# A four-layer network on one core: column sums added to the skip term by DMA, and the last experts in two halves

## The chip, the core and the metric

One core of a Trainium2 chip runs the whole program in one launch. The engines are PE (TensorE: matmuls), DVE (VectorE), ACT (ScalarE), POOL (GpSimd) and SP (SyncE, which here only issues DMAs). Each works through its own queue in order. The metric is the device time of one execution in microseconds (us), median of several runs.

## The reference, cut to what matters

The input x is 4 images of 64 x 64 positions with 128 channels. Four layers follow; each adds to x. Two are touched.

Layer 0 runs a selective scan over the 4096 positions of an image in four directions (rows, columns, and both backwards) for 256 inner channels with 16 states each, and sums the four results:

```python
xa = jax.nn.silu(xc)                       # after a 3 x 3 depthwise convolution
xs = jnp.stack([x_flat, x_t, jnp.flip(x_flat, 1), jnp.flip(x_t, 1)], axis=1)
ys = _selective_scan(xs, dts4, A, Bp4, Cp4, D_param, b_dt)   # each adds u * D_param
y = ys[:, 0] + transpose(ys[:, 1]) + flip(ys[:, 2]) + transpose(flip(ys[:, 3]))
y = layer_norm(y) * ln_w + ln_b
y = y * jax.nn.silu(z)
return y @ w_out
```

The four directions each add u times D_param, so their sum has a skip term of 4 D_param times xa. The column sums are the two transposed directions, the row sums the other two.

Layer 3 is a windowed attention with a layer norm, and then a mixture of 8 experts: router_probs = softmax(x @ router_w + router_b), the best two of eight are kept, and each token gets their weighted sum of x @ expert_w + expert_b.

## The kernel before

The program is written in the order of its Python code. Inside the layers' main loops the order on PE, ACT and DVE is the order of the code; POOL and SP are placed by a scheduler. A generator holds work that goes beside a main loop: each `yield` hands back to it.

**Layer 0.** The main loop has 512 steps: 4 images (b), 2 halves of the inner channels (h), 64 chunks (c) of 64 positions. A step does, for all four directions, the products (`products`, L641, PE, into three PSUM buffers db), the carry of the step before added to their first column (L654, DVE), four scans (L657, DVE; state in a buffer big), the carry for the next step (L665, POOL), the product with C over all states (L673, POOL, two per step), and the sum over the states (`total`, L686 on PE; with the results of the second half of the chunks, the direction that came first is added by L698). ACT copies the sums into two SBUF tiles (L705): yr for the two row directions, yc for the two column directions, each 128 x 4096 floats for one half of the channels. `inputs` (L632, DVE) prepares the next step and needs `delta` (L621, PE), which shares the tile aux with the sums. `fetch` loads ct, xo and dg for two steps ahead; SP issues these.

The row sums yr are written to DRAM eight chunks at a time (L710), once their second visit is through. A column chunk touches every row of yc, so yc goes out whole at the end of a half, in two writes of 1 MB (L714) to a DRAM tensor yc_d. yr and yc are single buffers.

Beside the loop of image b run, from chunk 4 of its first half, one after the other:

- `back(b - 1)`: 8 blocks of 512 positions. It loads the column sums yc, the skip term y0, the row sums yr and the gate zs (`fetched`, L459, 512 KB each, four buffers t4k), adds y2 += y0 (L468, POOL), y += y2 (L472, POOL), normalises, multiplies with the gate (L505, POOL), and projects (L512). The last image's `back` runs beside the beginning of layer 1.
- `front(b + 1)` and `middle(b + 1)`: group norm, input projection, convolution (L370), silu (L380, ACT, giving xh), the skip term y0 = xh * 4 D_param (L382, POOL, written to DRAM by L385), transposes and the scan's inputs. For image 0 these two run alone, ahead of the loop.

**Layer 3.** The main loop is the attention of the four images. Two lists of generators run beside it: `light` (the `front` and `back` of an image) and `heavy` (`chosen`, the router and experts of an image, two halves of 16 tiles each by `some`). `step` advances the first generator of a list. When an image's attention is done, `passed` runs its `back`, which writes blocks of t, and then appends that image's `chosen` to `heavy`; `chosen` of the last image comes after all else:

```python
            while light or heavy:
                step(light)
                step(heavy)
            for _ in chosen(B - 1, free_bank):
                pass
```

The router's logits are L2074, the experts' matmuls L2145, their weighted sums L2151 (DVE). `back`'s last operation of a block is L2037. Three kinds of PSUM banks are used: `own_bank` (tile x, one buffer), `shared_bank` (mm, two) and `free_bank` (s, two).

Of the kernel before, what the change touches and what calls it, by code (L numbers as in the profile page):

```python
# [15 lines left out]
B = 4  # L16
# [42 lines left out]
def tl(pool, shape, tag, dtype=F32, bufs=None):  # L59
    return pool.tile(shape, dtype, name=tag, tag=tag, bufs=bufs)  # L60
# [99 lines left out]
def layer0(cm, x, W, x1, also, kept):  # L160
# [5 lines left out]
    with ExitStack() as ctx:  # L166
# [93 lines left out]
        def begin(b):  # L260
            img[b] = {
                "zs": tl(dr, [P, 2, S], "zs"),
                "dl": tl(dr, [2, P, S], "dl_d"),
                "ct": tl(dr, [NST, S], "ct_d"),
                "xT": tl(dr, [2, S, P], "xT_d"),
                "y0": tl(dr, [P, 2, S], "y0_d"),
                "yr": tl(dr, [P, 2, S], "yr_d"),
                "yc": tl(dr, [P, 2, S], "yc_d"),
            }


# [87 lines left out]
        def middle(b, bank, pool, tag, ahead):  # L359

            ready = [shifted(i, pool, tag) for i in range(ahead)]
            for k in range(NBLK):
                cols = slice(k * BLK, (k + 1) * BLK)
                xa = []
                for h in range(2):
                    ps = bank()
                    x3 = ready.pop(0)
                    for dx in range(3):
                        for g in range(4):
                            nc.tensor.matmul(  # L370
                                ps[g * CG : (g + 1) * CG, :], lhsT=cdiag[:, 4 * h + g, dx, :],
                                rhs=x3[:, g, 0 : 8 * PADW].rearrange(
                                    "p (r w) -> p r w", w=PADW
                                )[:, :, dx : dx + HW],
                                start=(dx == 0), stop=(dx == 2),
                            )
                    if 2 * k + h + ahead < 2 * NBLK:
                        ready.append(shifted(2 * k + h + ahead, pool, tag))
                    xh = tl(tmp, [P, BLK], "t2k")
                    nc.scalar.activation(xh, ps, AF.Silu, bias=vec[:, 0, h : h + 1])  # L380
                    y0 = tl(tmp, [P, BLK], "t2k")
                    nc.gpsimd.tensor_tensor(  # L382
                        y0, xh, d4[:, h : h + 1].to_broadcast([P, BLK]), ALU.mult
                    )
                    nc.sync.dma_start(img[b]["y0"][:, h, cols], y0)  # L385
                    xa.append(xh)
                    yield
                    ps = bank()
                    for i in range(4):
                        nc.tensor.transpose(  # L390
                            ps[:, i * P : (i + 1) * P], xa[h][:, i * P : (i + 1) * P], cm.ident
                        )
                    t = tl(tmp, [P, 4, P], "t2k")
                    nc.scalar.copy(t, ps.rearrange("p (t c) -> p t c", c=P))
                    nc.sync.dma_start(
                        img[b]["xT"][h, cols, :].rearrange("(t p) c -> p t c", p=P), t
                    )
                    yield
                    if h == 0:
                        yield  # L400
                        yield
                ps = bank()
                n = RANK + 2 * NST
                for h in range(2):
                    nc.tensor.matmul(
                        ps[0:n, :], lhsT=w_xp[:, h, :], rhs=xa[h], start=(h == 0), stop=(h == 1)
                    )
                xd = tl(tmp, [P, BLK], "t2k")
                nc.scalar.copy(xd[0:n, :], ps[0:n, :])
                xr = tl(tmp, [P, 8, TC], "t2k")  # L410
                nc.scalar.copy(
                    xr[0:n], ps[0:n, :].rearrange("p (c t) -> p c t", t=TC)[:, :, ::-1]
                )
                nc.sync.dma_start(img[b]["ct"][:, cols], xd[RANK + NST : n, :])
                yield
                ps = bank()
                pb = ps[:, 0 : 8 * NST].rearrange("p (c n) -> p c n", n=NST)
                for c in range(8):
                    for j in range(2):
                        nc.tensor.matmul(  # L420
                            pb[j * TC : (j + 1) * TC, c, :],
                            lhsT=xr[0:n, c, :] if j else xd[0:n, c * TC : (c + 1) * TC],
                            rhs=cm.ident[0:n, RANK : RANK + NST], start=True, stop=True,
                        )
                nc.vector.tensor_copy(BT[:, 8 * k : 8 * k + 8, :], pb)
                for h in range(2):
                    yield


                    ps = bank()  # L430
                    nc.tensor.matmul(
                        ps, lhsT=w_dt[:, h * P : (h + 1) * P], rhs=xd[0:RANK, :],
                        start=True, stop=True,
                    )
                    bias = vec[:, 1, h : h + 1]
                    u = tl(tmp, [P, BLK], "t2k")
                    r = tl(tmp, [P, BLK], "t2k")
                    nc.scalar.activation(u, ps, AF.Abs, bias=bias)
                    nc.scalar.activation(r, ps, AF.Relu, bias=bias)
                    nc.scalar.activation(u, u, AF.Exp, scale=-1.0)  # L440
                    nc.scalar.activation(ps, u, AF.Identity, bias=cm.ones[:, 0:1])
                    v = tl(tmp, [P, BLK], "t2k")
                    nc.scalar.activation(v, ps, AF.Ln)
                    yield
                    nc.vector.scalar_tensor_tensor(
                        ps, ps, 1.0, u, ALU.subtract, ALU.subtract
                    )
                    nc.vector.tensor_tensor(ps, v, ps, ALU.subtract)
                    nc.vector.tensor_tensor(r, ps, r, ALU.add)
                    nc.sync.dma_start(img[b]["dl"][h, :, cols], r)  # L450
                yield

        def back(b, bank, tmp=tmp, t4=t4):


            def fetched(k, *names):
                ts = [tl(t4, [P, 2, BLK], "t4k") for _ in names]
                for t, name in zip(ts, names):
                    nc.sync.dma_start(t, img[b][name][:, :, k * BLK : (k + 1) * BLK])  # L459
                return ts  # L460

            y2, y0 = fetched(0, "yc", "y0")
            yield
            for k in range(NBLK):
                cols = slice(k * BLK, (k + 1) * BLK)
                xr = tokens(b, k, tmp)
                y, zl = fetched(k, "yr", "zs")
                nc.gpsimd.tensor_tensor(y2, y2, y0, ALU.add)  # L468
                yield
                yield  # L470
                yield
                nc.gpsimd.tensor_tensor(y, y, y2, ALU.add)  # L472
                if k + 1 < NBLK:
                    y2, y0 = fetched(k + 1, "yc", "y0")
                yield
                yield
                ps = bank()
# [202 lines left out]
        def total(I, part):  # L680
# [30 lines left out]
            if c == NCHUNK - 1:  # L711
                for r in range(2):
                    rows = slice(r * S // 2, (r + 1) * S // 2)
                    nc.sync.dma_start(img[b]["yc"][:, h, rows], yc[:, rows])  # L714

        def turn_bank():
            return tl(db, [P, BLK], "db")
# [886 lines left out]
def layer3(cm, W, M, cst, x2, out):  # L1604
# [6 lines left out]
    with ExitStack() as ctx:  # L1611
# [109 lines left out]
        def rows(a, b, k):  # L1721
            return a[b, k * BLK : (k + 1) * BLK, :].rearrange("(t p) c -> p t c", p=P)
# [273 lines left out]
        def back(b, bank):  # L1996
# [20 lines left out]
            for k in range(NBLK):  # L2017
# [18 lines left out]
                yield  # L2036
                nc.vector.tensor_tensor(t, t, xl, ALU.add)  # L2037
                nc.sync.dma_start(rows(me["t"], 0, k), t)
                if k + 1 < NBLK:
                    t, xl = block(x2, b, k + 1), block(me["xl"], 0, k + 1, "xl")  # L2040
                yield
# [131 lines left out]
        def passed(b, bank):  # L2173

            yield from back(b, bank)
            if b + 1 < B:
                heavy.append(chosen(b, own_bank))


        with tc.manual_schedule(engines={mybir.EngineType.PE}):  # L2180
            for _ in front(0, free_bank):
# [3 lines left out]
            for T in range(-AHEAD, LAST + 2):  # L2185
# [4 lines left out]
                for x in range(4):  # L2190
# [13 lines left out]
                    if x == 0 and 1 < T:  # L2204
                        divided(T - 2, 1)
                        b, m = divmod(T - 1, NM)
                        if m == 0:
                            merged(b - 1)
                            light.append(passed(b - 1, shared_bank if b < B else free_bank))
                            if b + 1 < B:  # L2210
                                fronts[b + 1] = front(b + 1, shared_bank)
                                light.append(fronts[b + 1])
# [3 lines left out]
                        weights(T, x // 2, x % 2)  # L2216
                    step(heavy)
                    step(light)
            while light or heavy:
                step(light)  # L2220
                step(heavy)
            for _ in chosen(B - 1, free_bank):
                pass


def hybrid_kernel(tc, I, cst, out):
# [86 lines left out]
```

## Time and profile before

| | |
|---|---|
| median of 3 runs | 11011.42 us (11002.11 to 11043.79) |
| the profiled execution | 11035.94 us, of which the span 11034.1 us |
| granted TensorE clock, mean | 0.892 |
| busy in the span: PE / DVE / ACT / POOL | 86% / 69% / 49% / 49% |
| scans L657 (DVE) | 2048 of 2286 ns |
| products L673 (POOL) | 1024 of 4538 ns |
| skip term L382 (POOL) | 64 of 1041 ns |
| adds L468 and L472 (POOL) | 32 each of about 2350 ns |

A span of 11 ms has stages with different limits: layer 0 fills the first 6430 us or so, layers 1 and 2 reach to about 9000, layer 3 takes the rest. A row of the page with a line gives engine, operation, out<-in, shapes and the count, then busy us and mean ns of one, then the idle time of the engine just before such instructions with what ended it.

### The profile page before, as it was taken

Reading aid. Unit: us, or ns where it says so; the run is one execution under the profiler, and the core shown is the slowest. Engines: PE = TensorE matmul, PEld = TensorE weight load, DVE = VectorE, ACT = ScalarE, POOL = GpSimd, SP = SyncE. Lnnn points to the kernel's source line nnn. Section 1 sums busy time; section 2 is a strip of 40 time slices with the busy share of each in tenths; the row PEclk is TensorE's granted clock in tenths of the full one; section 3 lists DMA queues with packets and bytes.
Section 4 is the critical chain, followed back from the end, with each engine's and each line's share of the span. In section 5 each row is a group of like instructions: output and inputs, shape, how many; then the busy total and the mean of one; then the engine's idle time right before and its main releaser. Section 6 shows DMA issues by size and latency. Waiting matters only on the chain. (4 is left out here: it accounts for less than half of the span.)

```text
span 11034.1 us, 163573 instructions
## 1 busy us (share of the span) xinstructions
PE 9541.3 (86%) x59368; PEld 4544.1 (41%) x59368; DVE 7577.1 (69%) x11174; ACT 5380.1 (49%) x13471; POOL 5453.8 (49%) x2661
## 2 busy tenths in 40 slices
PE   7789998889998889997889964999999966988886
PEld 2344444344443344443344432444444434544442
DVE  1898888888988888988899976645452122355546
ACT  5666443556444555445552223767777622343321
POOL 0678888878888888888889940000000000000000
PEclk7899999889998899998999976999999976677777
DMA  4334443334443334433333341111100065022101
GB/s 139 105 104 153 132 131 117 112 112 144 137 132 121 111 114 154 136 118 123 115 109 99 104 134 40 39 35 35 34 28 18 17 189 105 13 49 56 37 23 46
DMA packets 1479867, 1026.27 MB, mean 93 GB/s; under 512 B 698052, under 2 KB 1296808, under 8 KB 1474712
## 3 DMA queue, kind: packets, MB, share of 16 engines
q1 hardware_dynamic: 1479064, 1015.80, 31.0%
q8 instruction: 475, 7.78, 0.3%
q14 instruction: 328, 2.69, 0.1%
HBM read 683.79 MB, written 331.61 MB: 92 GB/s over the span
## 5 line engine op out<-in xcount | busy, mean ns | idle before, releaser
L657 DVE TENSOR_TENSOR_SCAN big<-dA,db 128x1024 f32<-128x1024 f32 x2048 | 4679.7, 2286 | 81.1 <-ACT dA L564 2.8
L673 POOL TENSOR_TENSOR big<-big,ct 128x2048 f32<-128x2048 f32 x1024 | 4647.0, 4538 | 84.5 <-DVE big L657 5.6
L641 PE MATMUL db<-dg,du 64*64 64x512 f32 x16384 | 2455.2, 621 | 98.3 <-DVE db L654 85.6
L686 PE MATMUL aux<-big,both 128*64 128x256 f32 x16384 | 2121.2, 403 | 466.1 <-DVE db L654 257.5
L686 PEld LDWEIGHTS aux<-big,both 128*64 128x64 f32 x16384 | 1207.8, 143 | 1466.8 <-issue 637.2
L705 ACT COPY yr<-aux 128x64 f32<-128x64 f32 x1024 | 226.2, 221 | 2773.2 <-PE aux L686 1316.5
L641 PEld LDWEIGHTS db<-dg,du 64*64 64x64 f32 x16384 | 748.2, 136 | 1329.1 <-issue 1225.9
L612 ACT ACTIVATE dg<-mask,BT 128x64 f32<-128x64 f32 x4096 | 1007.4, 341 | 4.8 <-DMA dg_d<-dg 4.8
L1443 PE MATMUL av<-e,x 128*128 128x512 f32 x2048 | 974.0, 592 | 4.6 <-ACT e L1438 4.6
L1394 PE MATMUL qk<-a,xT 128*128 128x512 f32 x2048 | 966.6, 594 | 8.7 <-ACT e L1398 7.9
L1398 ACT ACTIVATE e<-qk,nk 128x512 f32<-128x512 f32 x1024 | 693.2, 685 | 539.3 <-PE qk L1394 538.4
L564 ACT ACTIVATE dA<-dp,A 128x252 f32<-128x252 f32 x2048 | 870.6, 509 | 1.4
L973 POOL TENSOR_TENSOR g_rs<-g_rs,qrow 128x4 f32<-128x4 f32 x32 | 41.1, 1286 | 1499.8 <-DVE g_rs L972 1499.8
L665 POOL TENSOR_TENSOR cy<-big,a 128x32 f32<-128x32 f32 x1008 | 271.1, 269 | 758.7 <-DVE big L657 497.2
L1394 PEld LDWEIGHTS qk<-a,xT 128*128 128x128 f32 x2048 | 378.0, 190 | 462.3 <-issue 358.0
L1443 PEld LDWEIGHTS av<-e,x 128*128 128x128 f32 x2048 | 381.6, 190 | 434.8 <-issue 393.7
L1438 ACT ACTIVATE e<-e 128x1024 f32<-128x1024 f32 x510 | 538.8, 1056 | 15.5
L654 DVE TENSOR_TENSOR db<-db,cy 128x16 f32<-128x16 f32 x2016 | 336.2, 167 | 264.4 <-PE db L641 211.2
L1919 ACT ACTIVATE e<-s 72x576 f32<-72x576 f32 x448 | 273.6, 643 | 492.4 <-PE s L1912 489.6
L632 DVE TENSOR_TENSOR du<-xo,aux 128x128 f32<-128x128 f32 x1024 | 248.7, 283 | 346.3 <-PE aux L621 211.1
L1930 POOL COPY vp<-vt 72x160 f32<-72x160 f32 x56 | 20.2, 362 | 898.9 <-PE po L1936 896.2
L2151 DVE SCALAR_TENSOR_TENSOR tex<-x,gw,tex 128x128 f32<-128x128 f32 x768 | 264.4, 344 | 252.1 <-PE x L2145 237.0
(531 smaller groups left out, 11001.6 us busy)
## 6 DMA issues: line engine op xcount, KB each, us to landing
ct<-ct_d SPq DMA_DIRECT2D x1024, 128.0 KB
dg_d<-dg SPq DMA_DIRECT2D x256, 512.0 KB
dg<-dg_d SPq DMA_DIRECT2D x256, 512.0 KB
xo<-xT_d SPq DMA_DIRECT2D x2048, 32.0 KB
x<-xc_d SPq DMA_DIRECT2D x144, 264.0 KB
dp<-dl_d SPq DMA_DIRECT2D x256, 128.0 KB
t2k<-in_x SPq DMA_DIRECT2D x96, 256.0 KB
sp<-sp_d SPq DMA_DIRECT2D x16, 1280.0 KB
```

Of the source, the lines that this page charges most:

```text
L564: nc.scalar.activation(w["dA"][:, :, g, n, 1:], w["dp"][:, g, :, 1:], AF.Exp, scale=A[:, w["h"], g, n : n + 1],)
L612: nc.scalar.activation(q["dg"][:, n, :], mask, AF.Copy, scale=BT[:, q["c"], n : n + 1])
L641: nc.tensor.matmul(bs[j][p * TC : (p + 1) * TC, g * NH0 : (g + 1) * NH0, :], lhsT=q["du"][kp][half, g * TC : (g + 1) * TC], rhs=q["dg"][ha ...
L654: nc.vector.tensor_tensor(bs[j][:, :, 0], bs[j][:, :, 0], old[:, u, :], ALU.add)
L657: nc.vector.tensor_tensor_scan(st[:, u].rearrange("p n t -> p (n t)"), q["w"]["dA"][:, c % QC].rearrange("p g n t -> p (g n t)"), bs[j].re ...
L673: nc.gpsimd.tensor_tensor(sv, sv, q["ct"].rearrange("p n t -> p (n t)").unsqueeze(1) .to_broadcast([P, 4, NH0 * TC]), ALU.mult,)
L686: nc.tensor.matmul(yp[p * TC : (p + 1) * TC], lhsT=both, rhs=st[:, :, p * NH0 + n, :], start=(n == 0), stop=(n == NH0 - 1 and not late),)
L1394: nc.tensor.matmul(ps, lhsT=me["xT"][:, kt * P : (kt + 1) * P], rhs=me["a"][k], start=True, stop=True,)
L1398: nc.scalar.activation(e[:, j, :], ps, AF.Exp, bias=me["nk"][:, kt : kt + 1], scale=2.0)
L1438: nc.scalar.activation(es[g + 2], es[g + 2], AF.Exp)
L1443: nc.tensor.matmul(avs[b, k], lhsT=img[b]["x"][:, kt, :], rhs=e[:, j, :], start=(kt == 0), stop=(kt == NT - 1),)
L1919: nc.scalar.activation(e.rearrange("p j h q -> p j (h q)"), ss[p][0:HALF, :, 0 : 2 * WIN], AF.Exp, scale=0.5,)
```

## The change

In layer 0, the column sums are no longer written to a tensor of their own. GpSimd issues two accumulating DMAs of 1 MB that add yc onto the skip term y0 in DRAM, at the place in `total` where they were written. `back` loads y0 in place of both, and has one add. The skip term itself is made by ACT, as a copy with a scale for each partition.

In layer 3, `back` counts the blocks it has written in me["done"]. `last` goes into the heavy list once the main loop is through; it waits for half of the blocks of the last image, runs `some` on that half, and then does the same for the other. `back` of the last image takes its PSUM from `shared_bank` instead of `free_bank`.

```diff
@@ middle
-                    nc.gpsimd.tensor_tensor(
-                        y0, xh, d4[:, h : h + 1].to_broadcast([P, BLK]), ALU.mult
-                    )
+                    nc.scalar.activation(y0, xh, AF.Copy, scale=d4[:, h : h + 1])
                     nc.sync.dma_start(img[b]["y0"][:, h, cols], y0)
@@ back
-            y2, y0 = fetched(0, "yc", "y0")
+            (y0,) = fetched(0, "y0")
             yield
             for k in range(NBLK):
...
                 y, zl = fetched(k, "yr", "zs")
-                nc.gpsimd.tensor_tensor(y2, y2, y0, ALU.add)
                 yield
                 yield
                 yield
-                nc.gpsimd.tensor_tensor(y, y, y2, ALU.add)
+                nc.gpsimd.tensor_tensor(y, y, y0, ALU.add)
                 if k + 1 < NBLK:
-                    y2, y0 = fetched(k + 1, "yc", "y0")
+                    (y0,) = fetched(k + 1, "y0")
@@ total
             if c == NCHUNK - 1:
                 for r in range(2):
                     rows = slice(r * S // 2, (r + 1) * S // 2)
-                    nc.sync.dma_start(img[b]["yc"][:, h, rows], yc[:, rows])
+                    nc.gpsimd.dma_start(
+                        img[b]["y0"][:, h, rows], yc[:, rows], accum_op=ALU.add
+                    )
@@ layer 3, back
                 nc.sync.dma_start(rows(me["t"], 0, k), t)
+                me["done"] = k + 1
@@ layer 3
+        def last():
+            for half in range(2):
+                while img[B - 1].get("done", 0) < NB * (half + 1):
+                    yield
+                yield from some(img[B - 1]["t"], B - 1, NB * half, free_bank)
...
-                            light.append(passed(b - 1, shared_bank if b < B else free_bank))
+                            light.append(passed(b - 1, shared_bank))
...
+            heavy.append(last())
             while light or heavy:
                 step(light)
                 step(heavy)
-            for _ in chosen(B - 1, free_bank):
-                pass
```

## The prediction

> **What bounds the kernel now.** I first cut the span by stage. Layer 0 runs from 300 to about 6430 us, 58% of it. The page's slices show DVE and POOL as full as PE there, and two rows carry them:
>
> ```profile
> DVE  1898888888988888988899976645452122355546
> POOL 0678888878888888888889940000000000000000
> ...
> L657 DVE TENSOR_TENSOR_SCAN big<-dA,db 128x1024 f32<-128x1024 f32 x2048 | 4679.7, 2286 | 81.1 <-ACT dA L564 2.8
> L673 POOL TENSOR_TENSOR big<-big,ct 128x2048 f32<-128x2048 f32 x1024 | 4647.0, 4538 | 84.5 <-DVE big L657 5.6
> ```
>
> A step is four scans (9.1 us of DVE) and two L673 (9.1 us of POOL), so whatever delays either engine shows. Next, busy time by window: a stretch with nothing beside the scan, and one where `back` works on the image before (us, then PE, PEld, DVE, ACT, POOL busy):
>
> ```profile
> 5850.00:6350.00 500.00, 464.06 (x3496) 218.64 (x3496) 484.32 (x485) 110.63 (x444) 469.29 (x219) 1.00 0.33 101
> 2310.00:2346.00 36.00, 25.57 (x200) 13.10 (x201) 25.63 (x26) 15.11 (x63) 28.61 (x15) 0.86 0.34 110
> ```
>
> The plain stretch holds 195 scans, so a step takes 10.26 us and DVE idles 0.33 us in it. In the second DVE is busy for 25.6 of 36. What ends its idle time there is in the timeline of POOL and DVE:
>
> ```profile
> 2182.90 2.34 POOL L472 TENSOR_TENSOR t4k<-t4k 128x1024 f32<-128x1024 f32 x1 [4.37 <-DMA t4k<-yr_d]
> ...
> 2185.49 0.18 DVE L654 TENSOR_TENSOR db<-db,cy 128x16 f32<-128x16 f32 x1 [4.90 <-POOL cy L665]
> ...
> 2195.36 0.18 DVE L654 TENSOR_TENSOR db<-db,cy 128x16 f32<-128x16 f32 x1 [4.96 <-PE db L641]
> ```
>
> POOL is in order: L472 waits 4.37 us for its load, adds for 2.34, and the carry L665 behind it is late, so DVE waits. The second wait is the same delay by another way: L673 was late, hence PE's sums L686, and the products L641 queue behind those.
>
> Third, the steps where an image half ends (c = 1 and 2 of the next half):
>
> ```profile
> 2657.19 0.81 SPq L714 DMA_DIRECT2D yc_d<-yc  x2
> 2663.90 0.21 ACT L705 COPY yr<-aux 128x64 f32<-128x64 f32 x1 [11.39 <-DMA yr_d<-yr]
> 2668.80 0.27 ACT L705 COPY yc<-aux 128x64 f32<-128x64 f32 x1 [4.69 <-DMA yc_d<-yc]
> 2670.17 0.48 DVE L632 TENSOR_TENSOR du<-xo,aux 128x128 f32<-128x128 f32 x2 [9.47 <-PE aux L621]
> ```
>
> The next half may not overwrite yc before its 2 MB are out, and ACT, PE and DVE stand in line behind that. In the packet records, each 8 KB packet took 309 ns; all moved from 2661.4 to 2668.3.
>
> **What the Trainium skill says.** "DMA: Bandwidth & Descriptors", section "SWDGE vs HWDGE vs iDMA": an accumulating DMA can only be issued from GpSimd, whose software writes the descriptors. No DMA of POOL is in this trace. Same page, "SDMA does more than copy": the adder reduces two streams, 2048 elements at most. A row here has 2048; no run shows its speed. Same page, "Queues, rings and completion order": issuing engines have rings of their own, served in turn. The trace agrees as far as it goes: on SP's one queue, yc's packets waited 4 us behind earlier transfers.
>
> **The change, part by part.**
>
> *(a) One add of `back` less.* The order in which the changed program's instructions stand on POOL has the remaining add (y += y0) where L468 stood, except in an image's first two blocks (one step earlier, and L472's place of block 0). On SP, y0's load takes yc's place, yr's takes y0's, zs' takes yr's. So the remaining add waits for a load in L468's old position, behind the same ct loads: I keep L468's wait and drop L472 with its wait. Groups of instructions, 1800 to 5700 us (busy, mean ns, idle before):
>
> ```profile
> L468 POOL TENSOR_TENSOR t4k<-t4k 128x1024 f32<-128x1024 f32 x24 | 56.5, 2354 | 81.2 <-DMA t4k<-y_d 74.3 <-DMA xo<-xT_d 6.8
> L472 POOL TENSOR_TENSOR t4k<-t4k 128x1024 f32<-128x1024 f32 x24 | 56.3, 2346 | 32.2 <-DMA t4k<-yr_d 30.1 <-PE db L641 2.0
> ```
>
> Both hold POOL for 226 us over 24 blocks. DVE idles 194 us in the 36 steps that contain them; less 0.33 each, 182 are theirs, so 44 us (1.8 a block) are absorbed. Dropping L472's 88.5 frees 71 us in proportion, 88 if the slack is used up first. I take **-80**; the ends are -45 (only the adds go, since the later load rules) and -170 (both waits go: 56.5 less 44 stay).
>
> *(b) yc's write becomes 16 accumulating DMAs of 1 MB, by POOL.* They stand after the first L673 of c = 1, a step ahead of the stall. Two issues of an estimated 1 us (the skill's "Specifications" there gives this first-byte latency) delay the carry behind them, which is needed only after the stall: nothing. What counts is when yc comes free. In front of the second image's scan, SP issued the writes at 1823.6, the packets ran from 1829.1 to 1835.5, and ACT went on at 1836.4. In the new order POOL is free at 1825.5 (that step's L673), and an own ring need not wait behind yr and ct: data from about 1827.5. 16 rows for each of 16 engines: 4.9 us at 309 ns. The adder reads two streams, so I take twice the copy, 9.9 us; with 1.6 for sharing and 1.5 to completion, 1840.5, so +4 at each half. Seven such seams, and the end, where layer 1's first DVE instruction (L904) waits 20.2 us on yc's write: 8 x 4 = **+32**. Bounds: equal to a copy, -1 each (-8); five times a copy, 5 x 4 - 1 = +19 each (+152). Loads of y0 replace those of yc one for one in bytes; 24 of 512 KB fewer, against 16.8 MB read by the adder.
>
> *(c) The skip term by ACT.* 64 multiplications of 1.04 us leave POOL, 64 copies of about 0.63 us (row L488, same shape) join ACT. Per step of `middle` POOL has over 1 us free (busy 635 of 746 us, 2634 to 3380), nobody is listed as waiting for L382, and steps after one show no more DVE idle: 0. On ACT (busy 348 of those 746) the copy stands between L380 and a table load or L394; in the opening's 16 of them ACT idles 1.2 us there, waiting for PE's transposes. If that cover failed, 64 x 0.63 = +40. SP no longer stands 83 us in all before L385 for POOL, so ct and xo are issued earlier: **-5** (0 to -15).
>
> *(d) `back` of the last image, beside layer 1:* the same drop; PE waits 11.2 us for L472 there. **-6** (0 to -20).
>
> *(e) Layer 3.* `last` is behind `chosen` of image 2 in the heavy list, so it can begin early only if that ends before image 3's `back`. These two lines, one from the query of each source line, say no:
>
> ```profile
> L2037 DVE TENSOR_TENSOR tin<-tin,xl x32: 639/680/692, 9629.3 to 10845.4; 128x512 f32<-128x512 f32 x32
> ```
>
> ```profile
> L2145 PE MATMUL x<-ew,x3T x288: 592/697/1223, 10001.0 to 10855.9; 128*128 128x512 f32 x144
> ```
>
> `back` is through at 10845, the old experts run to 10856. In the changed order nothing of layer 3 moves on any engine; `back` merely writes bank mm instead of s, two buffers either way: **0** (3 either way).
>
> Sum: -80 + 32 - 5 - 6 = -59. The profiled execution took 11035.9 us (span 11034.1), 24.5 above the median 11011.4 of the runs; so 11035.9 - 59 = 10976.9 profiled, **10952** as a median. A measurement of this kernel tells about 0.5%, 55 us, from no change.
>
> **The rivals.**
> - *Both waits go.* With three tiles a block in four buffers, y0 and yr might land before POOL asks. For it: the boundary and the queue are less crowded. Against: the loads stand behind ct on SP, which waits on POOL. -170 + 32 - 11 = -149: 10862.
> - *The wait stays whole.* The one add waits for the later of two loads, and the shorter POOL queue arrives sooner and waits longer: -45 + 32 - 11 = -24: 10987.
> - *The adder is slow.* One row costs r copies; a seam moves by 5(r - 1) - 1 us. The 91 us gained in (a), (c) and (d) are spent at r = 3.5, and over that the kernel is slower, as ACT, PE and DVE all stand behind yc. r = 6: 8 x 24 = +192, so +101: 11112. For it: each row is read and written back in HBM beside the read from SBUF; against: rows of 8 KB are the largest here.
> - *Layer 3 does what its name says*: half of the tokens, about 85 us, would have to run under `back`. The order excludes it.
>
> **How the numbers follow.** Forecast 0.46, of which about 0.28 lies past -55 us (its own spread, from (a) at -71 to -88 and a seam of -1 to +9, is 10880 to 11000); both waits go 0.17; wait stays 0.13; slow adder 0.24, two thirds of it past +55, which begins at r = 4.9. So faster 0.28 + 0.17 = 0.45, slower 0.16, within 0.5% 0.39. The range takes in the second case nearly whole and the slow adder to r = 5 (+61): 10860 to 11070.
>
> **What would show it.** Right: 24 adds fewer on POOL in 1800 to 5700 us and the remaining one with 50 to 80 us of wait; steps with adds, now 16 to 20 us, fall by 3 on average; L632's waits at the seams grow from 5.4 to 9.8 us by about 4; packets of POOL's queue at some 620 ns; the time after 9000 us unchanged. Wrong: adder packets at 309 ns or above 1 us; DVE idle in the add steps unchanged; L2145 moved in the tail; ACT's copies with somebody waiting for them.

## The result, and the profile after

The changed kernel takes 10989.15 us (median of 20 runs; 11013.81 before): 0.9979 of the time before, 95% interval 0.9970 to 0.9989. That is 25 us less where 59 were forecast. The two profiled executions differ by 62 us, 10974.05 against 11035.94; most of that excess is scatter between single executions. The kernel with layer 3's part alone, which gains nothing in its median, has a profiled execution of 11011.80 us, 24 below that of before.

The page of the changed kernel, the two rows that fill layer 0, and the new queue:

```profile
L653 DVE TENSOR_TENSOR_SCAN big<-dA,db 128x1024 f32<-128x1024 f32 x2048 | 4680.0, 2286 | 82.1 <-ACT dA L560 3.2
L669 POOL TENSOR_TENSOR big<-big,ct 128x2048 f32<-128x2048 f32 x1024 | 4646.1, 4537 | 85.0 <-DVE big L653 5.4
...
q0 software_dynamic: 2304, 16.78, 0.7%
```

Scans and products are what they were. The queue of POOL's own DMAs holds the 16 accumulating ones, 16.78 MB. Busy time by window, a plain stretch and one around the last add of image 1 (us, then PE, PEld, DVE, ACT, POOL):

```profile
5800.00:6300.00 500.00, 462.97 (x3490) 218.04 (x3490) 483.87 (x488) 110.48 (x444) 468.99 (x221) 1.00 0.33 101
...
2283.00:2319.00 36.00, 31.67 (x241) 16.11 (x234) 29.87 (x32) 17.76 (x72) 31.24 (x16) 0.91 0.34 111
```

The plain stretch is unchanged. In the other, DVE is busy for 29.9 of 36 us, where it was 25.6. Groups of instructions, 1800 to 5700 us (busy, mean ns, idle before):

```profile
L468 POOL TENSOR_TENSOR t4k<-t4k 128x1024 f32<-128x1024 f32 x24 | 56.4, 2351 | 110.6 <-DMA t4k<-yr_d 80.4 <-issue 11.6 <-PE db L637 10.7
L501 POOL TENSOR_TENSOR t4k<-t4k 128x1024 f32<-128x1024 f32 x24 | 56.4, 2349 | 14.7 <-ACT t4k L497 14.7
```

24 adds are gone, but the 24 that remain wait 110.6 us, nearly as long as both kinds together did (113.4). The timeline at the second image's beginning (start, duration, then in brackets the idle time before and what ended it), before:

```profile
1823.59 0.90 SPq L714 DMA_DIRECT2D yc_d<-yc  x2
...
1836.40 0.27 ACT L705 COPY yc<-aux 128x64 f32<-128x64 f32 x1 [5.55 <-DMA yc_d<-yc]
...
1837.77 0.48 DVE L632 TENSOR_TENSOR du<-xo,aux 128x128 f32<-128x128 f32 x2 [6.40 <-PE aux L621]
```

And in the changed kernel:

```profile
1811.49 1.76 POOL L710 DMA_DIRECT2D y_d<-yc  x2
...
1828.73 0.27 ACT L701 COPY yc<-aux 128x64 f32<-128x64 f32 x1 [11.38 <-DMA y_d<-yc]
...
1830.10 0.48 DVE L628 TENSOR_TENSOR du<-xo,aux 128x128 f32<-128x128 f32 x2 [13.07 <-PE aux L617]
```

This seam (the step in which ACT waits for the write of yc at the start of a half) costs DVE 13.1 us, where it was 6.4. yc comes free 17.2 us after POOL issues, where it was 12.8 after SP did. The packet records of POOL's queue show 628 ns for each 8 KB packet (median), 2.03 times the plain write's 309. The tail, by source line:

```profile
L2035 DVE TENSOR_TENSOR tin<-tin,xl x32: 635/681/693, 9566.7 to 10783.3; 128x512 f32<-128x512 f32 x32
...
L2144 PE MATMUL x<-ew,x3T x306: 592/697/1222, 9899.7 to 10793.8; 128*128 128x512 f32 x153
```

The last operations of `back` and of the experts of the image before begin at 10783 and 10794 us, eleven microseconds apart as before. Layer 3 is what it was.

### The profile page after: what moved, and what is told of

Its sections match the earlier page's. It is cut to its first block, busy times and chain, and to the rows that moved or that the text cites. A ratio compares the mean times of both kernels' runs of the same rounds, so it can differ in the third digit from the quotient of the medians.

```text
span 10972.3 us, 163387 instructions
## 1 busy us (share of the span) xinstructions
PE 9474.1 (86%) x59368; PEld 4529.1 (41%) x59368; DVE 7569.2 (69%) x11174; ACT 5425.1 (49%) x13536; POOL 5331.9 (49%) x2581
## 3 DMA queue, kind: packets, MB, share of 16 engines
q0 software_dynamic: 2304, 16.78, 0.7%
```

## The experiments

Each kernel is compared with runs of the kernel before on its own chip (medians of before 11044, 11018 and 11027 us in the three groups), so a difference in us here is (1 - ratio) times that median. Step lengths are differences between the starts of every fourth scan. Images, blocks and steps are counted from 0, so that image 1 is the second; "over plain steps" means less 10.26 us.

**The skip term alone** (`middle` as in the change, all else as before).

> Only the skip term is moved from POOL to ACT; all else is the kernel before. Theory (from the two traces): the opening, where middle of image 0 runs alone, loses a round trip over POOL in each block, so the first scan begins near 282 us instead of 300 and the median falls by about 19 us; from the first scan to L904 nothing changes (6140 us, 3 either way). The prediction's view: the opening is unaffected, the whole change is worth 5 us. Rival: the 64 extra copies get in the way of ACT beside the scan, and the time from first scan to L904 grows by up to 40 us, so that the median is up to 20 us above before.

Measured: 1.0007 (0.9998 to 1.0016), 8 us more, in an interval that holds zero. My reading that the opening had become 19 us shorter falls: the first scan began at 279 us here, but at 282 us in the next kernel too, which leaves the skip term on POOL. The 300 us of the profile before were scatter: the single traces of later kernels began at 280 to 299 us with either engine.

**Layer 3 alone** (`last` and the bank).

> Only layer 3's part: last() in the heavy list, and back of the last image in bank mm. Theory: no instruction moves, so the median is that of before within 5 us and the time from L904 to the end is 4594 us, but for scatter of some 15 us. Rival: the changed kernel's profile is 20 us shorter from L904 to the end because of this part; then this kernel shows 10 to 20 us less in the median and in that stretch. Second rival: bank mm is shared with other work and costs, +10 to +20 us, which would explain why the median fell by 25 us only while layer 0 is 41 us shorter in the profile.

Measured: 1.0000 (0.9992 to 1.0008). No gain or loss is seen, to within 9 us. This kernel's layer 0 is that of before, so its trace serves as a second one of the old order. From the first DVE instruction of layer 1 to the end it took 4581 us (4594 and 4573 in the profiles before and after): that stretch scatters by 20 us and more.

**Column sums by DMA alone.**

> Only the accumulating DMA and the add that it saves; the skip term stays on POOL, layer 3 as before. Theory (sum over the steps of the two traces): the steps with adds give 88 us back, the seams and the end take 65, so first scan to L904 is 23 us shorter and the median about 23 us below before. Prediction's sizes: -80 + 32, 48 us below. Rival: the skip term on POOL stands in the way of the adds, and without its move the adds give less, the median is within 10 us of before.

Measured: 0.9979 (0.9969 to 0.9989), 23 us less: all that the changed kernel gains.

**One add fewer without the adder**, run in two groups. This kernel leaves the skip term y0 out of the sum, to save an add and a load without an accumulating DMA:

```diff
-            y2, y0 = fetched(0, "yc", "y0")
+            (y2,) = fetched(0, "yc")
...
-                nc.gpsimd.tensor_tensor(y2, y2, y0, ALU.add)
```

> The kernel before with yc written by SP as it was and back loading yc, yr and zs only: one add and one load of a block fewer, no accumulating DMA (the skip term y0 is left out of the sum). It shows the gain by itself. Theory: 88 us less from first scan to L904, the waits of L632 at the seams as before (5.4 to 9.8 us), median 80 to 95 us below before. Rival: only the time of the add itself is won, 45 us. Third: both waits go, 150 us or more.

> The kernel before with one add and one load of a block fewer, SP writing yc (the skip term y0 left out of the sum), once more for a closer number. The trace of its first run is 52 us shorter in the steps of layer 0 than three traces of the old order, its median was 73 us below before with a wide interval. Theory: where both adds stood in one step (three of eight blocks) nothing is won, since the carry waits for the first add and its load; so 55 to 65 us below before. The prediction's proportional share: 86 us below.

Measured: 0.9934 (0.9918 to 0.9951) and 0.9940 (0.9923 to 0.9957), 73 and 66 us less. Where it comes from is seen in the steps of image 2, first half (us):

```
step                                   2     4     5    11    17    22    28    33    39
old order (layer 3 alone)           17.6  19.3  19.7  16.1  18.8  16.0  19.6  16.1  18.8
one add fewer (second run)          19.4  11.5  20.0  16.2  13.3  16.0  14.9  16.1  13.4
column sums by DMA alone            25.1  19.3  10.3  16.4  15.3  18.5  13.4  16.0  13.1
```

Steps 4, 17, 28 and 39 held only the second add, and fall by 5 to 8 us each here (3 to 9 in all three images and both runs). Steps 5, 11, 22 and 33, with four of the eight blocks, held both, and win nothing. There the carry stands behind the first add and that add's load; the second add came later in the same step, into free time of POOL. Over the three images, steps 3 to 45 are 54 to 62 us shorter in all (the two runs against two traces of the old order). The add of block 2 in the second run's timeline:

```profile
3484.32 2.36 POOL L471 TENSOR_TENSOR t4k<-t4k 128x1024 f32<-128x1024 f32 x1 [4.53 <-DMA t4k<-yr_d]
3486.64 0.26 POOL L664 TENSOR_TENSOR cy<-big,a 128x32 f32<-128x32 f32 x1
```

Wait, add, and only then the carry L664: the order of both kernels in that step.

**The write by POOL, without the adder**: first with both adds, then with one, where the skip term is again left out of the sum.

```diff
-                    nc.sync.dma_start(img[b]["yc"][:, h, rows], yc[:, rows])
+                    nc.gpsimd.dma_start(img[b]["yc"][:, h, rows], yc[:, rows])
```

> The kernel before, with yc written to its own tensor by POOL instead of SP: the same place in the program as the accumulating DMA, without the adder. Theory: of the 51 us that the accumulating DMA adds at the seams, nearly all is the adder (packets of 628 ns for 309). Here packets take 309 ns again, the data starts some 3.5 us after POOL's issue, yc is free about 10.5 us after it (17 with the adder), L632 waits 5 to 10 us at the seams, and the median is that of before within 12 us. Rival: the way over POOL (late start, descriptors) is the cost; then the seams are as long as in the changed kernel (sum of the seven over plain steps near 109 us, 52 to 62 before) and the median is 40 to 50 us above before.

> The same (one add fewer, skip term left out), with yc's plain write issued by POOL at the place of the accumulating DMA. Three steps from here to the changed kernel: the way over POOL, then the adder. Theory now (from the plain write over POOL in the kernel before, which cost 45 us without any adder): the way over POOL is most of the cost, and this kernel is 25 to 45 us slower than the one with SP's write, within 15 us of the changed kernel's 25 below before. Rival: the adder's double time is the cost; then it is within 12 us of the one with SP's write.

Measured: 1.0041 (1.0030 to 1.0053), 45 us more, with both adds; but 0.9944 (0.9927 to 0.9960), 62 us less, with one. That is 4 to 11 us worse than SP's write, which the intervals don't tell from nothing. The first result seemed to put the whole cost on the way over POOL; the second has the adds in the changed kernel's steps, and gains more than it by 39 us, so most of the cost needs the adder. In the first kernel the scheduler had also moved the adds: steps 2 to 5 of image 2 take 21.0, 16.6, 21.0 and 17.2 us (17.6, 10.3, 19.3, 19.7 in the old order), some 9 us more in each of three images. Its first seam is 9 us longer as well; some 10 of the 45 us were not found. With one add the seams are 12 to 17 us longer than with SP's write (69 over plain steps for 52 and 57), but steps 4 and 5 together are 3 to 6 us shorter in each of the three images, since block 1's add has moved. The seam with one add and a plain write by POOL:

```profile
1818.14 1.13 POOL L713 DMA_DIRECT2D yc_d<-yc  x2
...
1829.93 0.27 ACT L704 COPY yc<-aux 128x64 f32<-128x64 f32 x1 [6.82 <-DMA yc_d<-yc]
```

yc is free 11.8 us after the issue, 17.2 with the adder. Over the seven seams, the data ends 12.1 us after POOL's first issue on average here, and 18.0 in the changed kernel: 5.9 us each, 41 in all. The seams over plain steps agree: 69 us here and 109 in the changed kernel. The medians put the adder at 39 us (62 less becomes 23 less, in two groups).

**Taking the wait for yc away.** A half's first two chunks put their column sums into a free t4k buffer; ACT copies them into yc with the third chunk's.

```diff
+            if c == 0:
+                room = tl(t4, [P, 2, BLK], "t4k").rearrange("p a s -> p (a s)")
+                side.append(room[:, 0 : 4 * TC].rearrange("p (k j t) -> p k j t", j=2, t=TC))
...
-                    nc.scalar.copy(vs[2 * j + kp], yj[:, ::-1] if j else yj)
+                    out = side[-1][:, c, j] if kp and c < 2 else vs[2 * j + kp]
+                    nc.scalar.copy(out, yj[:, ::-1] if j else yj)
+            if c == 2:
+                for cc in range(2):
+                    for j in range(2):
+                        nc.scalar.copy(views(yc, cc)[2 * j + 1], side[-1][:, cc, j])
+                side.pop()
```

> The changed kernel; the column sums of a half's first two chunks go to a side tile (in a free t4k buffer) and are copied into yc by ACT with the third chunk's, so that nothing asks for yc for some 20 us more. Theory: the seams' stall is ACT's wait for yc alone; of 109 us over plain steps at the seven seams at most 25 are left, and the median is about 80 us below the changed kernel (that is, some 105 below before). Rival: the stall moves to the next in line, the first add of back waiting for y0 behind the accumulation, or ACT's order; then 30 us or less is won.

> The kernel before with the same side tile. Theory: its seams hold 52 to 62 us over plain steps, of which some 40 go: median 40 us below before. The difference to the changed kernel with a side tile is then the worth of the saved add alone, 65 to 75 us (as the kernel with one add less and no adder showed: 73). Rival: the adder costs outside the seams too (traffic, first load of back); then that difference is under 45 us.

Measured: 0.9975 (0.9966 to 0.9984) on the changed kernel and 0.9979 (0.9969 to 0.9988) on the one before. The seams over plain steps fell from 109 to 29 us, yet the changed kernel won only some 3 to 5 us (28 below before, for 23 to 25), and stands no more than 5 us below the old order with the same side buffer, too little to be told from nothing. With short seams, too, the accumulation takes back nearly all that the saved add gives. The stall went to the next in line:

```profile
3400.07 2.34 POOL L468 TENSOR_TENSOR t4k<-t4k 128x1024 f32<-128x1024 f32 x1 [15.78 <-DMA t4k<-yr_d]
```

This is `back`'s first add of image 2, in step 3. SP could issue the load of y0 at 3386.1 only, when the first of the two accumulating DMAs was through, and yr's behind it. POOL stands 15.8 us, the carry behind it, and the step takes 27.2 us. Steps 3 to 5 of the three images together take 56 us more than in the changed kernel, of the 80 that the seams lost; the rest is not found.

**Loading earlier.**

```diff
-            (y0,) = fetched(0, "y0")
+            y0, y = fetched(0, "y0", "yr")
...
-                y, zl = fetched(k, "yr", "zs")
+                (zl,) = fetched(k, "zs")
...
-                    (y0,) = fetched(k + 1, "y0")
+                    y0, ahead = fetched(k + 1, "y0", "yr")
...
+                y = ahead
```

> The changed kernel, where back loads the row sums of a block together with its y0, right after the add of the block before, instead of at the block's beginning (four buffers are enough with three tiles a block). Theory: the remaining add waits 110 us in 24 blocks for the later load, which stands behind ct and xo on SP; loaded earlier most of the wait goes (30 us left) and, as DVE idles 126 us in those steps, 50 to 70 us of the time. Rival: the wait is not for yr but for y0, or for the scheduler's place of the add on POOL, and less than 15 us is won.

Measured: 0.9979 (0.9970 to 0.9988), as the changed kernel; the wait of L468 is still 104.8 us. SP issued block 2's load of y0 in image 2 at 3493.2, just after the gate L501 of block 0 (3490.8), whose operand frees a buffer; the scheduler's order has the add two steps after that gate, where it waited 6.2 us more. Code that asks earlier changed neither.

**POOL in the order of the code**, without and with the side buffer:

```diff
         engines = {mybir.EngineType.PE, mybir.EngineType.Activation, mybir.EngineType.DVE}
+        engines.add(mybir.EngineType.Pool)
```

> The changed kernel, with POOL's instructions in layer 0 in the order of the code instead of the scheduler's. Theory: the scheduler puts the remaining add as early as the buffers allow, right behind the issue of its load, so POOL waits for the load (110 us in 24 blocks) and the carry stands behind it; in code order the add comes one and a half steps after its loads, the wait falls under 25 us, the steps with adds lose 60 to 90 us, and the median is as much below the changed kernel. Rival: the wait appears elsewhere (the gate L501 then waits for ACT in front of a carry, or the carry for the add), and less than 20 us is won.

> The changed kernel with the side tile and with POOL in code order. With the side tile alone the seam's stall went to the first add of back, which the scheduler had put a step after the seam, behind y0's load. Theory: with the add in code order that load has landed; the seams hold under 25 us over plain steps (109 in the changed kernel), and the median is 110 to 150 us below the changed kernel. Rival: only the sum of one of the two edits is seen, 50 to 80 us, since the stall finds another place.

Measured: 0.9918 (0.9903 to 0.9933), 90 us below before; with the side buffer 0.9842 (0.9825 to 0.9858), 174 us below (10851.05 us): this beats both kernels. The groups of the first, 1800 to 5700 us:

```profile
L501 POOL TENSOR_TENSOR t4k<-t4k 128x1024 f32<-128x1024 f32 x24 | 56.7, 2362 | 0.0
L468 POOL TENSOR_TENSOR t4k<-t4k 128x1024 f32<-128x1024 f32 x24 | 56.5, 2353 | 0.0
```

The adds are as many and as long as in the changed kernel, and wait for nothing. Together the two edits win more than apart (174 us, for 90 and 28): the side buffer's stall had moved to the very wait that the code order takes away. What is left of seams with both, 36 us over plain steps, lies mostly at two, where ACT waits for yr's write (21.9 and 17.7 us). No run has the kernel before in code order, so what one add fewer is worth without these waits stays open.

## Why the prediction missed

The direction was right, and the two main terms were the ones that count. The forecast was the difference of these two large terms, and by the medians each was mis-sized by some 15 us in the same direction.

- **(a), with (d).** Forecast -80 and -6, measured -66 and -73 (the ends of their intervals -47 and -91, so the medians alone hardly tell them from the forecast). The steps do: 54 to 62 us for (a). The step that failed is the proportional share, which gave 71 as the least: the DVE idle time of the add steps was divided between L468 and L472 by their time on POOL. The table shows that half of the blocks' second adds, those in one step with a first add, had no share at all. The premise beneath it held: in the kernels with one add fewer the remaining add sits in the old first add's steps and keeps its wait (88.5 and 82.9 us, where L468 had 81.2 and 90.7 in two traces of the old order), and carries behind it wait. (d) alone is too small to be read against a scatter of 20 us in that stretch.
- **(b).** Forecast +32, measured about +47 (from 66 to 73 less to 23 less), of which 39 the adder. Twice the copy per packet, an estimate from the Trainium skill's statement that the adder reduces two streams ("DMA: Bandwidth & Descriptors", section "SDMA does more than copy"), was right to 2%; that reading the second stream is what doubles it, no run shows. The step that failed is +4 for each of seven seams, taken from the second image's: the seven stood 52 to 62 us over plain steps in traces with SP's write, and 109 in the changed kernel, so they grew by 47 to 57 for a forecast of 28. The estimate for the start, from that page's "Specifications" (1 us to the first byte), gave data 2 us after POOL came free; the eight accumulations began 2.6 to 6.1 us after the first issue. So a queue of POOL's own brought less than forecast: its plain writes, too, began 1.2 to 5.3 us after the issue, SP's 1.3 to 5.5 us in the trace of before. The accumulations then took 11.8 to 14.1 us, where 9.9 and 1.6 for sharing were forecast; only the 1.5 us to completion were too long (0.5 in the second image). In the second image the stall grew by 6.7; the very first seam, which was short before (ACT waited 2.1 us for yc), now stops DVE for 15.1 us. The end, L902, waits 28.1 us (20.2 before).
- **Beside (b), not foreseen.** `back`'s first load stands behind the accumulation, and its first add waits 8.6 to 10.4 us in the three images (0 to 1.6 in the first run with one add fewer). This wait falls into the seam's own stall and adds little: with POOL in code order, where this add comes later, the three seams are 0.4 to 1.5 us shorter. (The loads of 512 KB that are gone are 32 in all, 16.8 MB less read from HBM, not 24.)
- **(c).** Forecast -5, measured +8 with an interval that holds zero. SP's earlier issues bought nothing that can be seen, and the copies on ACT cost nothing that can be: the changed kernel, which has them, gains 25 us, and the one with the column sums alone 23.
- **(e).** Forecast 0; measured 1.0000. The order said so.
- **Rivals.** "Both waits go" and "the slow adder" did not come (r = 2.03). "The wait stays whole" gave 10987, and the wait did stay: 110.6 us, where 50 to 80 were named as the sign of being right. But its reason was another, since without the adder the wait was 82.9 to 88.5; the rest is mostly the first block's load behind the accumulation. The number agrees by its sum, which is luck, not by its parts: it set (a) at -45, and one add alone is worth about 70.
- **From profile to median.** The profiled executions differ by 62 us, the forecast's 59 nearly; taken alone they would have confirmed it. The medians of 20 runs say 25. Single traces began layer 0's loop anywhere from 279 to 300 us, and the time after it ran from 4563 to 4612 us over all the traces. This scatter goes with PE and its clock: in that stretch the same 18264 matmuls kept PE busy for 3825 us in the shortest trace and 3865 in the longest, and the changed kernel's runs go from 10970 us at a mean granted clock of 0.898 to 11025 us at 0.893.

## What to carry over

Where two adds stood in one step, the carry waited for the first, and removing the second won nothing: look at each step's order, not at shares of busy and idle time, and find the steps that hold both. An in-order engine placed by a scheduler may stand right behind a load's issue; putting it in the code's order was worth more here (67 us) than the whole change (25 us). When a wait is taken away, ask who else stands behind the same transfer: most of the seams' 80 us came back in the steps of the next adds until those were moved too.

## What was not expected of the hardware

The data of POOL's DMAs began 2.6 to 6.1 us after the first accumulating issue, and 1.2 to 5.3 us after the first plain one, later in most cases than the 2 us taken. POOL was held 1.8 us by the second image's two accumulating issues, 1.1 us by its two plain ones. In the changed kernel SP waited with `back`'s first load of y0, and with yr's behind it, for the first accumulating DMA, and issued it some 12 to 13 us after POOL began.
